# Moving the mask transposes from TensorE to a transposing DMA, the small start loads to GpSimd's queue, and adding a branch hint, in a two-layer graph kernel

## The chip, the cores and the metric

The kernel runs on one core of a Trainium2 chip, in one launch. The metric is the device time of a run in microseconds (us). Engines are named as the profile names them: PE is TensorE (matrix products and transposes), PEld its weight loads, DVE is VectorE, ACT is ScalarE, POOL is GpSimd and SP is SyncE, which here only issues DMAs. A q behind an engine's name (SPq, POOLq) marks what its sequencer does by itself: issuing a DMA, a branch, a wait.

## The reference

There are 64 graphs (B) of 256 nodes (N) with 256 features (D), and an integer mask `adj` per graph, drawn as 0 or 1. Two layers run one after the other on `x`:

```python
x = x + _L0_gnn_ref(_layernorm(x), adj, W, a)          # graph attention under the mask
x = x + _L0_ffn_ref(_layernorm(x), W_in, conv_w, ...)  # a Mamba-2 block: projection, conv, scan, gate, W_out, W_lin
x = x + _L1_gnn_ref(_layernorm(x), adj, adj, weight, bias)   # relational sum: masks (adj == r) @ x, times weight[r]
x = x + _L1_ffn_ref(_layernorm(x), gate_w, ...)        # mixture of 8 experts, one per token, with a capacity
```

The mask is used twice. The attention wants it with a target node on each partition (the way it lies in memory); the relational sum needs it with the source node on the partitions, so each 128x128 block of it has to be transposed. In the relational sum a value r of `adj` selects `weight[r-1]`; with a mask of zeros and ones only relation 1 ever occurs.

## The kernel before, in words

The program is written twice: a fast form that assumes that the mask holds only 0 and 1, and a slow, general form for any integers. The fast form sums up a test of the mask in `tested` while it runs; at the end `again` says whether the general form must run, and an `If` (L1844) skips it otherwise. With these inputs it is skipped.

Each form has two passes.

**First pass.** `prepare` (L583) loads and combines weights: `win` (the Mamba input projection), `wx` (attention weights with extra columns), `wf` (W_out times W_lin with routing columns), `wrel`. The helpers `centred` (L510) and `projected` (L526) do this by PE products whose results DVE (L522, L550) or ACT (L538) copies out of PSUM. `smaller` (L563) loads nine small parameter vectors (`cw`, `cb`, `aneg`, `dtb`, `dch` twice, `blin`, `brel`, `gb`) by DMAs that ACT issues (L566); DVE then halves `cw` and `cb` (L572), and ACT and DVE turn `aneg` into minus its exponential (L638, L639). `clear_slots` (L717) fills the routing table `slots` by another DMA from ACT (L721).

Then 32 groups follow, each of two graphs, which is 512 tokens in four tiles of 128. `group` (L1562) is `attention`, `scan`, `mix`, `relate`, and after every second group `choose`, which routes tokens to experts. In `attention` ACT makes `hide` (L947), a bf16 tile of 128x1024 that is 0 where there is an edge and -2^53 where there is none. In `mix` the same tile, there called `entries`, is transposed by PE, eight 128x128 blocks a group in two steps of four (L1270), into PSUM, and ACT squares and scales it into `adjT`, a 0/1 matrix (L1280). `relate` multiplies by it (L1340, through the helper line L871).

The engines' order in the fast first pass is not the program's order. Every piece of work is a step of a planner (`Plan`, L143): an engine, an estimated duration, what it reads and writes, and for DMAs a latency (`late`) and a time on the shared transfer (`move`). `Plan.record` (L230) simulates the five engines and emits the steps in the order that comes out; ties of start times go by a due time from the tables `DUE` (steps of a group) and `LATE` (steps before and after the groups). Each engine then works through its list in order, so a step that waits holds everything behind it on that engine. SP's list holds the loads of `x` and `adj`, the round trips through DRAM that spread rows over partitions (`s2d` L975/L979, `sumd` L1137, `spread` L1145) and the stores.

```python
            if found is None or t < found[0] - 0.05 or (
                t < found[0] + 0.05 and step.rank < found[1].rank
            ):
                found = (t, step)
```

Near the end of the groups three expert blocks (`first_block`, L1443) fill gaps.

**Second pass** (L1624). Experts' tokens are worked on in blocks of 512 (`wholes`) and of 128 (`quarters`), as many of each as a count found at run time says. Blocks are a nest of `If`s (L1814) inside one another; each block near its end marks a branch hint for the next block's `If` (L1818) on PE, ACT and DVE (`LEAPS`). Before the blocks POOL gathers tokens for the first ones: whole block 0, whole block 1, quarter blocks 0 and 1 (L1807 to L1809), and DVE normalizes quarter block 0 (`ahead`, L1810). Here engines follow the program's order.

Of the kernel before, what the change touches and what calls it, by code (L numbers as in the profile page):

```python
# [20 lines left out]
P = 128  # L21
# [15 lines left out]
    -26698, -26684, 16811, 5376, -1385, 22233, -9147, -5334, -6104, 16470, -4131, -12656,  # L37
    -16678, -3231, 6549, -17865, 6326, -26892, -31112, -17903, -11408, -796, -4422, -12203,
    -5594, 1406, -16327, -16058, -1084, -23798, -1397, -15584, 5401, -4898, -4435, 935, -15679,
    -4926, -36182, -30952, -7116, -5042, -13894, -12081, -3776, -29694, -776, -6149, -737,  # L40
    -14378, -1040, -15690, -8132, 2125, -13292, -19871, -13259, -19271, -17469, 3004, -3551,
    4598, 2717, -5807, -3518, -9626, -6760, -8973, -6760, -21580, -11090, -13187, -7075, -11614,
    8090, 12562, -15384, -25650, -16843, -17448, -16224, -33117, 17100, -11357, -1083, -673,
    -3047, -34625, -12261, -11942, 2714, -6609, 1789, 18383, -20000, 539, -3738, -33183, 333,
    14191, 6307, -9703, 30905, -7622, -19413, -14996, -28968, 116, 19317, 13445, 26060, -32817,
    248, -10405, 2927, -14690, 5944, -2080, -8721, 12774, 2204, -13729, 4024, -22409, -14504,
    5811, -7220, 1399, 13432, 6555, 4744, 7244, -13074, -17598, 12021, -2116, 1124, 383, 10928,
    4031, 2410, 19564, 20208, -4179, 14906, 17031, 1067, -9078, 28505, -6557, -15751, 31775,
    11208, -2943, -655, 18912, 7874, -12175, -12506, -31318, 19350, -32822, -27902, -1902,
    -2614, -22515, -11078, -32731, -7356, 9498, -25579, 6544, -6873, -12295, -8836, -15217,  # L50
    -101, -7100, 1503, -1212, -9384, -7250, 7131, 13184, 2367, 8234, -705, 2385, 15949, -10902,
    -6702, -11680, 4975, -8597, -19533, -14786, 2673, 6442, -7886, -3758, -14584, -18956, -2394,
    6472, -5117, -11835, -8654, 5355, -7098, 108, -26795, -19293, 8894, -21711, 8534, -22778,
    -5174, -16079, -18727, 6779, -14626, -18887, 15787, 204, 5445, -8225, -16055, 4780, 11196,
    -12432, -7396, 2489, -34797, 6092, -3614, -2035, -16485, -22244, -7928, 6163, -16171,
    -13402, 1393, 27308, -3299, 5434, 7440, -6001, 3226, -22066, 7952, -6124, -10687, 10110,
    -11601, -18846, 4084, -3318, -15991, -8790, -25459, 1833, -3473, -2961, -9107, -8293,
    -10502, -18974, -9710, -22513, -11406, -10557, -20206, -7421, -19897, -8699, -9302, -1570,
]
LATE = [  # L60
    -64053, -54702, -59145, -54915, -60062, -63895, -58481, -57817, -56638, -54542, -53887,
    -59553, -60544, -66295, -55138, -53590, -62371, -50547, -58476, -56411, -63929, -54771,
    -63020, -60249, -57757, -55870, -61971, -61584, -58713, -56315, -59515, -60412, -56997,
    -64050, -63593, -58710, -64327, -56974, -64548, -58677, -56261, -55764, -60770, -59294,
    -62214, -59216, -59275, -59000, -57674, -55104, -55629, -58061, -56012, -54911, -56448,
    -55347, -53242, -55651, -59000, -49001, -50233, -59769, -51850, -47995, -48427, -58143,
    -60315, -52513, -54188, -52953, -54782, -51621, -54327, -55185, -53707, -51746, -57084,
    -60544, -52244, -51134, -55346, -54169, -51215, -49728, -43803, -49582, -50567, -47711,
    -54575, -51840, -56142, -59770, -49885, 1346, -2673, -2320, -6355, -808, -6495, -5278,
    -5282, -4565, -4966, -834, -2200, -5069, -7821, -3201, -6160, -4309, -4527, -4910, -2257,  # L70
    -8341, -9201, -6505, -7591, -10768, -9145, -8325, -8954, 8280, 735, 3335, -7607, 7899, 6405,
    7444, -13853, 1045, -3011, 6416, -58, -9653, 9740, 2791, 9305, -3096, 1595, 7797, -2202,
    7339, -6677, 1395, 1189, 3316, 8270, 4320, 8345, 5395, -1209, 1024, 496, 4166, -5572, 10007,
    984, -7144, -1767, -9049, 430, 8168, 10157, 6125, 715, 2433, 5530, 2682, 9681, 4044, -3041,
    -2968, 5666, 3203, 7815, 2227, 4671, 4049, -972, 4835, -9096, 753, -943, -2244, 8804, -7176,
    9169, -3264, 14310, -351, -5008, 8557, -1420, 9011, 5402, 779, 9849, 8608, 3319, 8980, 5929,
    -754, -2251, 3474, -6957, 7127, 2274, 10247, -3481, 49, -3510, -403, -1726, 3946, 2006,
    -1802, 6377, 976, 1673, 5692, 3521, 6, -7831, -15890, 3058, 4170, -7076, 10709, 9000, 6424,
    5864, 2733, 2629, -4870, -702, -2673, 634, -1458, 1299, -687, 5733, -4310, 3394, -1918, 941,
    7852, -2182, 5064, -1684, 13692, 2798, 396, 8917, -2630, 8846, 9132, -2375, 11666, 11022,  # L80
    2337, 10279, 5111, 2075, -596, 5177, -3671, 3927, 3650, 11368, -4611, -3648, -135, -7000,
    2097, 4479, -1495, -2818, 6266, 3575, 372, 3192, -53, 1241, -9215, -13160, 8371, 1767,
    -8809, 9253, 10686, 2871, 6318, 5744, 6064, -7776, -3563, -2652,
# [59 lines left out]
class Plan:  # L143
# [6 lines left out]
    LEFT = 30  # L150

# [34 lines left out]
    def step(self, engine, us, go, reads, writes, late=0.0, port=0, move=0.0):  # L186
        k = self.k.get(self.due, 0)
        self.k[self.due] = k + 1
        due = (DUE if self.due == "group" else LATE)[k]
        step = Step(engine, us, go, self.g, self.TAIL[engine] + late, PACE * self.g + due,  # L190
# [128 lines left out]
def gnn_mamba_rgcn_moe(ctx: ExitStack, tc: tile.TileContext, a: dict, out: bass.AP):  # L319
# [33 lines left out]
    def row(ap):  # L353
        return ap.rearrange("(o d) -> o d", o=1)
# [33 lines left out]
    ident_b = const.tile([P, P], BF16, name="ident_b")  # L388
    nc.vector.tensor_copy(ident_b, ident)
# [92 lines left out]
    def first_pass(form, pass1):  # L482
# [80 lines left out]
        def smaller(s):  # L563

            def load(us, move, dst, src, home):
                s.step(ACT, us, lambda: nc.scalar.dma_start(out=dst, in_=src), [], [home], late=1.5, move=move)  # L566

            dskip = a["L0_ffn_D"].rearrange("(c q) -> q c", q=2)
            load(0.5, 0.2, cw, a["L0_ffn_conv_w"].rearrange("(c p) k -> p c k", p=P), s.fixed(cw))
            load(0.5, 0.2, cb, a["L0_ffn_conv_b"].rearrange("(c p) -> p c", p=P), s.fixed(cb))  # L570
            for half in (cw, cb):
                s.step(DVE, 0.1, lambda half=half: nc.vector.tensor_scalar(  # L572
                    half, half, 0.5, None, ALU.mult), [], [s.fixed(half)])
            load(0.5, 0.1, aneg, row(a["L0_ffn_A_log"]).broadcast_to([P, NH]), s.fixed(aneg))
            load(0.5, 0.1, dtb, row(a["L0_ffn_dt_bias"]).broadcast_to([P, NH]), s.fixed(dtb))
            for q in range(2):
                load(1.4, 0.1, dch[q * 64 : (q + 1) * 64, :], dskip[q : q + 1, :].broadcast_to([64, NCT]),
                     (s.fixed(dch), q))
            load(0.5, 0.5, blin[:, 0:D], row(a["L0_ffn_b_lin"]).broadcast_to([P, D]), (s.fixed(blin), "d"))
            load(0.5, 0.5, brel[:, 0:D], row(a["L1_gnn_bias"]).broadcast_to([P, D]), (s.fixed(brel), "d"))  # L580
            load(0.5, 0.1, gb, row(a["L1_ffn_gate_b"]).broadcast_to([P, E]), s.fixed(gb))

        def prepare(s):  # L583
# [36 lines left out]
            for i in range(2):  # L620
# [4 lines left out]
            s.step(DVE, 0.1, lambda: nc.vector.tensor_copy(gq0()[:, :, E + 1 :], win[:, :, DPROJ - NH :]),  # L625
                   [(win_, "dt")], [(two_, "q2")])
# [11 lines left out]
            s.step(ACT, 0.2, lambda: nc.scalar.activation(aneg, aneg, AF.Exp), [], [rate_])  # L638
# [78 lines left out]
        def clear_slots(s, homes):  # L717

            blank = s.tile("dm", [P, E * CAPP * 4 // P], bufs=4)
            s.step(POOL, 0.7, lambda: nc.gpsimd.memset(blank(), FAR), [], [blank])  # L720
            s.step(ACT, 0.5, lambda: nc.scalar.dma_start(  # L721
                out=slots.rearrange("(p j) w -> p (j w)", p=P), in_=blank()), [blank], homes, late=2.0, move=1.2)
# [457 lines left out]
        def mix(s, g, xe, entries, full, dt, gate, xh, bm, cm, dec):  # L1180
# [82 lines left out]
            adjT = []  # L1263
            for bi in range(2):
                ps, at = s.psum(BF16), s.tile("adjT", [P, 512], F32R, bufs=3)

                def turn(bi=bi, ps=ps):
                    for k in range(2):
                        for h in range(2):
                            nc.tensor.transpose(  # L1270
                                ps()[:, k * N + h * P : k * N + (h + 1) * P],
                                entries()[:, 2 * bi + h, k * P : (k + 1) * P],
                                ident_b,
                            )
# [349 lines left out]
    def second_pass(form, pass2):  # L1624
# [180 lines left out]
        for i in range(2):  # L1805
            quarters.fetch_weights(i)
# [76 lines left out]
```

## Time and profile before

| what | value |
|---|---|
| time, median of 3 runs | 2338.86 us (2333.72, 2338.86, 2339.75) |
| the profiled execution | 2332.68 us; its span from first to last instruction 2331.0 us |
| busy share of the span: PE, PEld, DVE, ACT, POOL | 96%, 67%, 75%, 71%, 39% |
| mean granted TensorE clock | 0.987 |
| moved by DMA | 274.71 MB, mean 118 GB/s |
| first pass | 0 to about 1765 us; steady groups from 60 to 1450 us, 50 us a group |
| second pass | whole blocks to about 2257 us, six quarter blocks to 2310 us |

The page of a profile lists busy times, the span in 40 slices, DMA queues, the chain of work that ended last, and the costliest groups of instructions with the idle time before them and who ended it. Further views of the trace answer narrower questions: who waited for whom, one line's or one tile's instructions, busy times by stage, and instructions in order of time. Matmuls overlap each other, so the duration of one is longer than the step from one to the next.

### The profile page before, as it was taken

How to read it: one execution, taken by the hardware profiler on the slowest of the kernel's cores; microseconds unless marked ns; L12 is line 12 of the kernel's file. 1: busy time of each engine (PE TensorE's matmuls, PEld its weight loads, DVE VectorE, ACT ScalarE, POOL GpSimd, SP SyncE). 2: the span in 40 equal slices, each digit the busy share in tenths (PEclk: the TensorE clock that was granted, in tenths of full speed). 3: DMA queues.
4: the chain of work that ended last, by engine and by line, in shares of the span. 5: the costliest groups of instructions: out<-in, count | busy, mean ns of one | idle time of the engine just before them, and what ended most of it. 6: DMA issues, size and time to landing. Idle time of an engine off the chain costs nothing.

```text
span 2331.0 us, 34861 instructions
## 1 busy us (share of the span) xinstructions
PE 2232.1 (96%) x11079; PEld 1558.4 (67%) x11079; DVE 1757.0 (75%) x4396; ACT 1665.1 (71%) x3864; POOL 919.7 (39%) x994
## 2 busy tenths in 40 slices
PE   5999999999999999999999999999998999999996
PEld 4676766667676666766766667656665666666675
DVE  3899999999999998999998998799654434333342
ACT  3899999899999899999999988888632222222223
POOL 1233435354453445445354444533635222222221
PEclk7999999999999999999999999999999999999998
DMA  4333445444444445444444444424527333333336
GB/s 135 95 90 107 112 117 126 110 108 108 116 121 128 110 102 115 120 118 126 110 108 108 110 123 117 111 67 113 158 81 242 122 119 113 114 117 117 114 92 194
DMA packets 200022, 274.71 MB, mean 118 GB/s; under 512 B 28505, under 2 KB 165919, under 8 KB 199809
## 3 DMA queue, kind: packets, MB, share of 16 engines
q1 hardware_dynamic: 149968, 211.48, 28.9%
q0 software_dynamic: 46848, 58.91, 13.8%
q8 instruction: 93, 1.52, 0.3%
q10 hardware_dynamic: 2992, 1.81, 0.2%
q14 instruction: 121, 0.98, 0.2%
HBM read 187.70 MB, written 46.04 MB: 100 GB/s over the span
## 4 chain that ended last, share of the span: by engine, by line
PE 40%; issue 20%; ACT 12%; POOL 11%; DVE 10%; DMA 5%; SPq 0%; POOLq 0%; ACTq 0%; DVEq 0%
PE ps L871 26%; PE ps L1240 4%; POOL slots L1436 3%; POOL out_dram L477 3%; POOL xg L455 3%; ACT dm L1158 2%; DVE y L1098 2%; PE ps L910 2%; PE ps L1244 2%; PE ps L1543 1%; ACT dm L1164 1%; DMA x<-in_x_dram 1%; DVE dm L1232 1%; ACT xh L1256 1%; ACT xn L925 1%
## 5 line engine op out<-in xcount | busy, mean ns | idle before, releaser
L871 PE MATMUL ps<-xnT,win 128*128 128x512 f32 x1152 | 542.0, 597 | 4.8 <-ACT xnT L915 3.8
L1158 ACT ACTIVATE dm<-spread,cs 128x256 f32<-128x256 f32 (+1 forms) x1024 | 379.3, 452 | 22.6 <-PE ps L1244 22.6
L1098 DVE SCALAR_TENSOR_TENSOR y<-ps,cw,y 128x510 f32<-128x510 f32 (+2 forms) x480 | 351.5, 738 | 34.6 <-ACT y L1091 31.8
L871 PEld LDWEIGHTS ps<-xnT,win 128*128 128x128 f32 x1152 | 205.9, 190 | 171.6 <-issue 150.8
L1744 PE MATMUL ps<-w,hid 128*128 128x256 f32 x1184 | 263.3, 380 | 0.0
L871 PE MATMUL ps<-wf,gate 128*128 128x265 f32 x1024 | 250.8, 388 | 0.0
L1744 PEld LDWEIGHTS ps<-w,hid 128*128 128x128 f32 x1184 | 224.2, 191 | 37.0 <-issue 8.1
L1730 PE MATMUL ps<-xnT,w 128*128 128x512 f32 (+1 forms) x704 | 246.8, 509 | 1.5 <-ACT xnT L1711 1.5
L1232 DVE TENSOR_TENSOR dm<-dm,bc 128x1536 f32<-128x1536 f32 x128 | 225.2, 1760 | 2.5 <-ACT dm L1164 2.4
L871 PEld LDWEIGHTS ps<-wf,gate 128*128 128x128 f32 x1024 | 190.3, 190 | 45.2 <-issue 11.7
L1734 ACT ACTIVATE hid<-ps,b 128x512 f32<-128x512 f32 (+1 forms) x184 | 110.4, 604 | 129.4 <-PE ps L1730 126.1
L1730 PEld LDWEIGHTS ps<-xnT,w 128*128 128x128 f32 x704 | 120.6, 193 | 118.3 <-issue 111.0
L1164 ACT ACTIVATE dm<-dm 128x1536 f32<-128x1536 f32 x128 | 190.5, 1490 | 0.0
L1436 POOL DMA_INDIRECT slots<-meta,sl x128 | 153.8, 1201 | 50.6 <-issue 31.5
L1240 PE MATMUL ps<-dm,xdt 128*64 128x256 f32 x1024 | 169.4, 391 | 3.6 <-DVE xdt L1221 2.9
L889 DVE BATCH_NORM_STATS2 st<-x 128x6 f32<-128x256 f32 x384 | 155.2, 413 | 1.5 <-DMA x<-in_x_dram 1.3
L879 POOL TENSOR_SCALAR ve<-mv 128x4 f32<-128x4 f32 x96 | 36.6, 382 | 300.6 <-DVE mv L892 186.1
L1749 DVE SCALAR_TENSOR_TENSOR yv<-ps,meta,bp 128x256 f32<-128x256 f32 x50 | 24.2, 484 | 160.7 <-PE ps L1744 150.0
L871 PE MATMUL ps<-wrel,hr 128*128 128x265 f32 x512 | 136.1, 395 | 2.0 <-ACT hr L1349 0.5
L871 PE MATMUL ps<-wx,xT 128*128 128x292 f32 x512 | 134.9, 409 | 0.0
L1711 ACT COPY xnT<-ps 128x512 f32<-128x512 f32 (+1 forms) x48 | 21.4, 496 | 152.4 <-PE ps L1708 152.4
L871 PE MATMUL ps<-wh,eT 128*128 128x273 f32 x512 | 126.9, 395 | 0.5 <-ACT eT L1016 0.5
(311 smaller groups left out, 4845.1 us busy)
## 6 DMA issues: line engine op xcount, KB each, us to landing
spread<-sumd SPq DMA_DIRECT2D x128, 512.0 KB, 4.0
w<-in_L_ffn_w_dram SPq DMA_DIRECT2D x50, 1024.0 KB, 6.0
x<-blin POOLq DMA_DIRECT2D x32, 530.0 KB, 5.7
x<-brel POOLq DMA_DIRECT2D x32, 530.0 KB, 5.7
x<-in_x_dram SPq DMA_DIRECT2D x32, 512.0 KB, 5.3
adji<-in_adj_dram SPq DMA_DIRECT2D x32, 512.0 KB, 4.6
out_dram<-x SPq DMA_DIRECT2D x32, 512.0 KB, 3.0
x3d<-x SPq DMA_DIRECT2D x32, 512.0 KB, 6.1
```

The source lines that it names most:

```text
L455: nc.gpsimd.indirect_dma_start(out=dst, out_offset=None, in_=source, in_offset=bass.IndirectOffsetOnAxis(ap=col, axis=0),)
L871: nc.tensor.matmul(out_, lhsT=lhsT, rhs=rhs, start=(i == 0), stop=(i == len(pairs) - 1))
L889: s.step(DVE, 0.34, lambda j=j: nc.vector.bn_stats(sb()[:, j, :], src()[:, j, 0:D]), [(src, j)], [(sb, j)])
L1098: nc.vector.scalar_tensor_tensor(y3[:, :, d:], p3[:, :, : N - d], cw[:, c, k : k + 1], y3[:, :, d:], ALU.mult, ALU.add,)
L1158: nc.scalar.activation(dm()[:, q, bi, o : o + n], spr()[:, q, t1 - n : t1], AF.Relu, bias=cs()[:, 4 * h + j : 4 * h + j + 1], scale=-1.0,)
L1164: s.step(ACT, 1.38, lambda: nc.scalar.activation(dm(), dm(), AF.Exp, scale=-1.0), [], [dm])
L1232: s.step(DVE, 1.67, lambda dm=dm: nc.vector.tensor_mul(dm(), dm(), bc().unsqueeze(1).to_broadcast([P, 2, 2, N + P])), [bc], [dm], port=1)
L1240: nc.tensor.matmul(o, lhsT=xdt()[:, 2 * bi, h * 64 : (h + 1) * 64], rhs=dm()[:, q, bi, 0:N], start=True, stop=False,)
L1436: s.step(POOL, 1.1, lambda j=j: apart("slots", nc.gpsimd.indirect_dma_start(out=slots, out_offset=bass.IndirectOffsetOnAxis(ap=sl()[:, j : ...
L1730: nc.tensor.matmul(ps[:, :n], lhsT=w1[:, k, f * P : (f + 1) * P], rhs=turned[:, k, :], start=(k == 0), stop=(k == 1),)
L1734: nc.scalar.activation(hid[:, f, :], ps[:, :n], AF.Relu, bias=self.b1[i % 2][:, f : f + 1])
L1744: nc.tensor.matmul(ps[:, :D], lhsT=hid[:, f, j * P : (j + 1) * P], rhs=w2[:, f, :], start=(f == 0), stop=(f == NFT - 1),)
```

## The change

Five things change; the rest of the kernel stays.

1. The mask's transposes. The two PE steps a group go, with the PSUM banks they used and the bf16 identity `ident_b`. In their place SP issues one transposing DMA a group from `entries` to a new bf16 tile `turned` in SBUF (one buffer), and ACT's squaring reads `turned` instead of PSUM.
2. The nine small loads go to GpSimd's queue. Halving `cw` and `cb` and the exponential of `aneg` now come after `wx` in their dependences, and so does the DMA that clears `slots`. The columns of `W_in` for `dt` are loaded by a small DMA of their own from SP (in place of a DVE copy out of `win`).
3. The planner counts a PE step 2.2% longer (`SLOWER`), and both tables of due times are new. So the order of all steps of the first pass may differ.
4. In the second pass the gather for whole block 1 is issued before that for whole block 0.
5. Every executed quarter block of the fast form also marks a hint for the general form's branch, as likely taken, on PE, ACT and DVE.

```diff
+    SLOWER = 1.022
...
+        us *= self.SLOWER if engine == PE else 1.0
...
-    ident_b = const.tile([P, P], BF16, name="ident_b")
-    nc.vector.tensor_copy(ident_b, ident)
...
             def load(us, move, dst, src, home):
-                s.step(ACT, us, lambda: nc.scalar.dma_start(out=dst, in_=src), [], [home], late=1.5, move=move)
+                s.step(POOL, us, lambda: nc.gpsimd.dma_start(out=dst, in_=src), [], [home], late=2.0, move=move)
...
-            for half in (cw, cb):
-                s.step(DVE, 0.1, lambda half=half: nc.vector.tensor_scalar(
-                    half, half, 0.5, None, ALU.mult), [], [s.fixed(half)])
...
-            s.step(DVE, 0.1, lambda: nc.vector.tensor_copy(gq0()[:, :, E + 1 :], win[:, :, DPROJ - NH :]),
-                   [(win_, "dt")], [(two_, "q2")])
+            load(0.3, lambda: gq0()[:, :, E + 1 :],
+                 a["L0_ffn_W_in"][:, DPROJ - NH :].rearrange("(k p) o -> p k o", p=P), (two_, "q2"))
...
-            s.step(ACT, 0.2, lambda: nc.scalar.activation(aneg, aneg, AF.Exp), [], [rate_])
+            for half in (cw, cb):
+                s.step(DVE, 0.1, lambda half=half: nc.vector.tensor_scalar(
+                    half, half, 0.5, None, ALU.mult), [wx_], [s.fixed(half)])
+            s.step(ACT, 0.2, lambda: nc.scalar.activation(aneg, aneg, AF.Exp), [wx_], [rate_])
...
-                out=slots.rearrange("(p j) w -> p (j w)", p=P), in_=blank()), [blank], homes, late=2.0, move=1.2)
+                out=slots.rearrange("(p j) w -> p (j w)", p=P), in_=blank()), [blank, s.fixed(wx)], homes,
+                   late=2.0, move=1.2)
...
-            adjT = []
+            adjT, turned = [], s.tile("turned", [P, 2, 2, 2, P], BF16)
+            s.step(SP, 0.4, lambda: nc.sync.dma_start_transpose(
+                out=turned().rearrange("p b h k n -> p (b h k) n"),
+                in_=entries().rearrange("p j n -> p (j n)")), [entries], [turned], late=2.0, move=1.2)
             for bi in range(2):
-                ps, at = s.psum(BF16), s.tile("adjT", [P, 512], F32R, bufs=3)
...
-                s.step(PE, 0.24, turn, [entries], [ps])
...
+                def square(bi=bi, at=at):
+                    out_ = at().rearrange("p (k h n) -> p k h n", k=2, h=2)
+                    in_ = turned()[:, bi].rearrange("p h k n -> p k h n")
...
+                        nc.scalar.activation(
+                            out_, in_, AF.Square, scale=-1.0 / NEG_BIG, bias=one,
+                            accum_out=tested[:, g, 1 + bi : 2 + bi])
...
+        wholes.gather(1, nc.gpsimd)
         wholes.gather(0, None)
-        for blocks, i in ((wholes, 1), (quarters, 0), (quarters, 1)):
-            blocks.gather(i, nc.gpsimd)
+        for i in range(2):
+            quarters.gather(i, nc.gpsimd)
...
                     def hint(k=k, i=i + 1):
+                        if form == "fast" and k:
+                            tc.mark_branch_hint_location("general", "LikelyTaken", engines=LEAPS)
...
-                here.enter_context(tc.If(again > 0))
+                here.enter_context(tc.If(again > 0, label="general"))
```

The two tables of numbers (`DUE` and `LATE`) are left out of the diff; all of their rows are new.

## The prediction

> **What bounds the kernel now.** I read first the busy times of all engines by stage.
>
> ```profile
> core 0: us, PE busy (x) PEld busy (x) DVE busy (x) ACT busy (x) POOL busy (x), PEclk, DMA share, GB/s
> 0.00:16.00 16.00, 7.59 (x20) 4.14 (x20) 2.17 (x20) 0.00 (x0) 2.95 (x17) 1.00 0.54 154
> 16.00:23.00 7.00, 0.00 (x0) 0.00 (x0) 1.97 (x7) 1.49 (x2) 0.00 (x0) 0.70 0.64 189
> 23.00:37.00 14.00, 13.64 (x61) 13.17 (x62) 6.23 (x28) 3.33 (x8) 1.36 (x2) 0.50 0.57 184
> ...
> 60.00:1450.00 1390.00, 1362.24 (x7401) 953.91 (x7400) 1279.92 (x3034) 1265.85 (x3014) 610.31 (x654) 1.00 0.44 112
> 1450.00:1765.00 315.00, 301.50 (x1464) 207.68 (x1463) 238.66 (x620) 213.63 (x499) 140.24 (x148) 0.99 0.42 114
> ```
>
> From 60 to 1450 us PE is busy 98% of the time, DVE 92%, ACT 91%: PE bounds the groups, and only 27.8 us of its time there is waiting. DMA is busy 44%. The start is another matter: for 7 us PE does nothing, then runs at half clock. The waits of the first 60 us say why:
>
> ```profile
> ACT L638 <- DMA cw<-in_L_ffn_conv_w_dram: 19.5, 1, 19.5
> DVE aneg L639 <- ACT aneg L638: 10.7, 1, 10.7
> ...
> PE ps L533 <- DVE gate L522: 8.2, 1, 8.2
> ```
>
> ACT computes nothing before 19.5 us: its list begins with eleven DMA issues, the last of which ends at 19.47 us by the timeline. DVE's list has `aneg` (L639) early, so it stands 10.7 us behind ACT, and the centring copies (L522) behind that make PE wait 8.2 us.
>
> Then the steps that the change takes away, by their line:
>
> ```profile
> L1270 PE MATMUL ps<-ident_b,hide x256: 216/219/230, 46.1 to 1668.6; 128*128 128x128 bf16 x128
> ```
>
> In the timeline a step of four starts 0.234 us before the next step of PE, in nearly all of the 64. And two places of the second pass, the wait at its entry and the branch over the general form:
>
> ```profile
> DVE xn L461 <- DMA xg<-x3d,place: 18.7, 1, 18.7
> ```
>
> ```profile
> L1842 PEldq COMPARE_BRANCH  x1: 4492/4492/4492, 2311.4 to 2311.4; - x1
> ...
> L1842 POOLq COMPARE_BRANCH  x1: 50/50/50, 2319.4 to 2319.4; - x1
> L1842 POOLq INC_SWDGE_SEM  x1: 1597/1597/1597, 2322.5 to 2322.5; - x1
> ```
>
> **The change, part by part.** The sum is made against the profiled execution, 2332.68 us (span 2331.0). The median of the runs, 2338.86, is 6.2 above it; I carry the difference over.
>
> *Mask steps off PE.* 64 x 0.234 = 15.0 us of PE. PE is the bound where they stand, and its successor stands ready almost always (waits 2%). DVE and ACT keep 8 to 9% of room, against 0.47 us of 50 (0.9%) that a group gets shorter. Bounds: 0 (something else sets the pace) and -15.0. I take 7/8 of it, -13, since in the late stage PE waits 4% already.
>
> *What replaces them.* ACT's squaring stays, 64 instructions; it now reads SBUF. The row is L1280, 684 ns from PSUM, against L1256, the same function on 128x512 from SBUF, 632 ns: at most 3 us less on an engine that isn't the bound, counted at nothing. SP gets 32 transposing DMAs of 256 KB. No row shows one. The nearest is `s<-s2d`, also 256 KB onto 128 partitions: issued in 0.34 us, landed in 3.1. The far end is the loads of single 4-byte elements (`dch`: 0.67 us to issue, 8.2 to land for 1 KB). I take the near row, since the operation moves whole tiles. Cover: in steady groups `hide` is done 100 us before PE's first mask step of that group (238.3 against 340.8 us in group 5), so a latency of 3 or of 10 us is hidden alike. It is not hidden from SP's list: behind the transpose stand the loads of `x` and the `s2d` and `spread` trips, and PE waits for `x` six times already between 60 and 1450 us (6.0 us in all). Traffic: 8.4 MB more, on 275, with the engines 44% busy. Taken as 0; the other end is in the second rival.
>
> The Trainium skill ("VectorE: DVE Perf Modes", section on the three transpose paths) speaks against the move: it gives 390 ns for a 128x128 bf16 block on TensorE and 1309 ns by the DMA crossbar, and advises TensorE where PSUM will do. This trace has 0.234 / 4 = 0.06 us a block as PE steps it, even cheaper; no run here shows the crossbar. By the page's figure, an estimate, eight blocks in a row would be 10.5 us a group, under the cover above, and the sum would stay the same unless SP is held meanwhile.
>
> *Small loads to POOL.* ACT loses nine issues, and `clear_slots` moves behind `wx`. POOL gets nine DMAs; its one plain DMA row (L701) is 1.13 us, so 10.2 us, in a stretch (3.6 to 31.8 us) where POOL waits 28.2 us for L701's data. So they end near 14 us; `cw`, `cb`, `dtb` are first needed in the first scan, after 60 us. If that cover were gone, POOL's next step (L879, 36.8 us) would be late by the rest. The extra `dt` load costs SP one issue of 0.37 us and takes a DVE copy of 0.18 us that waited 5.8 us for `win`. With ACT free and `aneg` behind `wx`, DVE's 10.7 us of waiting and with it PE's 8.2 us go, unless the loads of `x` come late: the first is issued at 13.1 us, and PE uses it at 36.3. Bounds: 0 (the new order puts another wait there) and -8.2 by this row; if the clock also held, PE's 16 us at half clock (23 to 39 us) could lose up to half, 7 to 8 more, so -16. I take -8.
>
> On that last item the skill ("TensorE: Matmul & The Clock Gate", part 1) says that an idle window of about 3.4 us halves the clock. The rows agree: PE rests from 15.2 to 23.4 us and its granted clock is 0.50 afterwards. By that rule the start would give the whole -16; I hold to -8, as other short waits may do the same.
>
> *The new order.* Tables and `SLOWER` change every tie. The trace can't show the new waits; it can bound them: all of the 27.8 us gone, or as much again, so -28 to +28. I take 0, and this is the widest term.
>
> *Gather order.* DVE's 18.7 us wait at the second pass's entry is for quarter block 0's gather (`ahead`, L1810), which is the ninth of ten before and after. Whole block 1's rows come four gathers (4 x 1.27 = 5.1 us) earlier, but their normalization stands behind `ahead` on DVE. So 0; -5 if `ahead` is not what it waits for.
>
> *Hint.* Six quarter blocks ran. A hint costs 28 ns on PE (23 of them stand in the trace already): 6 x 0.03 = 0.2 us. What could it give? PE spends 4.49 us in the branch (L1842), but PE, ACT and DVE are through at 2316.4, 2317.5 and 2320.5 us, and POOL, which gets no hint, branches at 2319.4, goes on at 2322.0 and drains to 2330.1. POOL sets the end, so the gain is 0. The far side: if each early hint pushes out code that the next block needs, up to 4.49 us a block, 27 us.
>
> Sum: -13 - 8 + 0.2 = -20.8. 2332.7 - 20.8 = 2311.9, on the median's scale 2338.9 - 20.8 = **2318**.
>
> **Rivals.**
> - *The PE time goes into waits* (no change). The group's pace is taken over by DVE and ACT, or the new order waits 15 to 20 us more, inside the bound of +28. For it: DVE and ACT at 92% and 91%. Against: 8% is much more than 0.9%. Time: -20.8 + 18 = -3, some 2336.
> - *SP becomes the place of the loss* (slower). A transpose holds SP's list, or the DMA rings behind it, longer than 0.34 us, and the `x`, `s2d` and `spread` transfers behind it come late to PE. It decides from 20.8 / 32 = 0.65 us of PE waiting a group. At 2 us a group it is +64, so 2338.9 - 20.8 + 64 = 2382; at the 8 us of the small-element row held each time, +256. For it: no row shows the operation, and PE already waits for `x`. Against: SP spends most of its time waiting, and the 100 us of slack lets the planner place it anywhere.
> - *The hint hurts*: +27 at most on top, 2345. Against: 23 hints in the trace, with whole blocks at 100% PE from 1800 to 2245 us; but those name branches that are mostly not taken.
> - *Better than forecast*: the clock holds at the start and all of the mask steps count: -15 - 16 = -31, 2308; with a good order below 2303.
>
> **How the numbers follow.** The measurement can tell about 0.3%, 7 us. Forecast, including the better case, 2300 to 2331: 0.61. Waits, 2332 to 2346: 0.13. SP, or the hint, above 2346: 0.26. The likeliest case alone would be 2302 to 2331. Leaving out 5% below and 15% above gives 2302 to 2362. Faster 0.61, same 0.13, slower 0.26.
>
> **What would show it.** Right: L1270 gone, groups 49.5 to 49.7 us apart instead of 50.1; ACT's first instruction before 5 us, PE's first group product (L871, now 42.2 us) near 34; SP's new issues under 0.5 us; the span's end still on POOL. Wrong: PE waits for `x`, `s` or `spread` in each group; SP issues of several us; the period unchanged with more PE waits; quarter blocks longer than 7.8 us apart.

## The result, and the profile after

The changed kernel takes 2342.91 us (median of 20 runs) against 2336.44 us of the kernel before (20 runs): a ratio of 1.0032, 95% interval 1.0024 to 1.0040. It is 7 us slower, where 21 us less was forecast. The profiled execution has a span of 2341.0 us (2331.0 before).

Busy time by stage, kernel after; the columns are PE, PE's weight loads, DVE, ACT and POOL busy in us, the granted clock, the DMA share and GB/s:

```profile
core 0: us, PE busy (x) PEld busy (x) DVE busy (x) ACT busy (x) POOL busy (x), PEclk, DMA share, GB/s
...
16.00:23.00 7.00, 6.25 (x47) 5.71 (x46) 4.80 (x22) 2.00 (x7) 0.90 (x1) 0.95 0.89 296
23.00:37.00 14.00, 11.28 (x54) 9.60 (x54) 6.92 (x26) 7.44 (x16) 3.23 (x7) 0.90 0.56 167
...
60.00:1450.00 1390.00, 1348.74 (x7093) 933.21 (x7093) 1306.64 (x2989) 1252.40 (x2987) 610.87 (x645) 0.99 0.47 116
```

At the start PE works from 16 to 23 us, where it did nothing before, and its clock is 0.90 instead of 0.50 from 23 to 37 us. In the first 60 us there is one long wait of PE in the group steps, for ACT's `ev`, which was 5.6 us before:

```profile
PE ps L1011 <- ACT ev L1000: 9.6, 1, 9.6
```

From 60 to 1450 us PE has less work, as foreseen, but the work takes longer to pass: DVE is busy 26.7 us more with almost the same instructions. Where the time went is best seen in the times at which stages begin (first matrix product of the stage in each trace, us from the span's start; "old order" is the whole change with the steps in their old order, `all_old_order` below):

| stage begins | before | after | whole change, old order |
|---|---|---|---|
| group 0 (its first decay sum, L1126 before) | 76.2 | 63.1 | 72.7 |
| group 4 | 235.1 | 230.7 | 230.9 |
| group 24 | 1236.1 | 1246.0 | 1230.9 |
| first whole block | 1764.1 | 1780.4 | 1757.3 |
| second whole block | 1802.8 | 1811.8 | 1796.8 |
| first quarter block | 2261.8 | 2272.9 | 2256.2 |
| end of the span | 2331.0 | 2341.0 | 2323.1 |

The period is the distance from group 4 to group 24, divided by 20: 50.05 us before, 50.77 us after, 50.00 us with the old order. All periods below are made in this way. The distances alternate (46.0 and 53.7 us before), so a pair of groups, some 100 us, is the unit in which work repeats.

The transposing DMA has a row of its own, from the instructions of its line (minimum, median and maximum of its issue on SP's list, in ns):

```profile
L1266 SPq DMA_TRANSPOSE turned<-hide x32: 1252/2024/3894, 32.1 to 1645.8; - x32
```

At the end, the branch over the general form is no shorter for PE (5.2 us, 4.49 before); POOL branches last, 0.2 us behind DVE:

```profile
L1845 PEldq COMPARE_BRANCH  x1: 5203/5203/5203, 2324.2 to 2324.2; - x1
...
L1845 POOLq COMPARE_BRANCH  x1: 50/50/50, 2331.7 to 2331.7; - x1
```

### The profile page after: what moved, and what is told of

It is laid out like the page before. It is cut to its first block, busy times and chain, and to the rows that moved or that the text cites. A ratio compares the mean times of both kernels' runs of the same rounds, so it can differ in the third digit from the quotient of the medians.

```text
span 2341.0 us, 34444 instructions
## 1 busy us (share of the span) xinstructions
PE 2233.4 (95%) x10823; PEld 1545.8 (66%) x10823; DVE 1802.1 (77%) x4394; ACT 1662.8 (71%) x3864; POOL 933.4 (40%) x1003
## 5 line engine op out<-in xcount | busy, mean ns | idle before, releaser
L1100 DVE SCALAR_TENSOR_TENSOR y<-ps,cw,y 128x506 f32<-128x506 f32 (+2 forms) x480 | 354.3, 741 | 28.3 <-ACT y L1093 26.3
L1234 DVE TENSOR_TENSOR dm<-dm,bc 128x1536 f32<-128x1536 f32 x128 | 235.1, 1836 | 7.0 <-ACT dm L1166 6.0
L873 PEld LDWEIGHTS ps<-wf,gate 128*128 128x128 f32 x1024 | 196.3, 194 | 65.9 <-issue 19.8
L881 POOL TENSOR_SCALAR ve<-mv 128x4 f32<-128x4 f32 x96 | 51.7, 538 | 321.8 <-DVE mv L894 320.4
L891 DVE BATCH_NORM_STATS2 st<-x 128x6 f32<-128x256 f32 x384 | 150.1, 416 | 6.9 <-DMA x<-in_x_dram 6.2
L873 PE MATMUL ps<-wx,xT 128*128 128x292 f32 x512 | 145.8, 422 | 0.0
L873 PE MATMUL ps<-wh,eT 128*128 128x273 f32 x512 | 132.6, 402 | 3.6 <-ACT eT L1018 3.5
L873 PE MATMUL ps<-wrel,hr 128*128 128x265 f32 x512 | 130.6, 392 | 3.6 <-ACT hr L1349 2.9
L1093 ACT ACTIVATE y<-ps,cb,cw 128x512 f32<-128x512 f32 x160 | 123.6, 772 | 10.7 <-PE ps L873 10.5
```

Of the source, the lines that this page charges most:

```text
L873: nc.tensor.matmul(out_, lhsT=lhsT, rhs=rhs, start=(i == 0), stop=(i == len(pairs) - 1))
L891: s.step(DVE, 0.34, lambda j=j: nc.vector.bn_stats(sb()[:, j, :], src()[:, j, 0:D]), [(src, j)], [(sb, j)])
L1093: s.step(ACT, 0.66, lambda: nc.scalar.activation(y(), ps(), AF.Identity, scale=cw[:, c, 3:4], bias=cb[:, c : c + 1]), [ps, s.fixed(cw), s. ...
L1100: nc.vector.scalar_tensor_tensor(y3[:, :, d:], p3[:, :, : N - d], cw[:, c, k : k + 1], y3[:, :, d:], ALU.mult, ALU.add,)
L1234: s.step(DVE, 1.67, lambda dm=dm: nc.vector.tensor_mul(dm(), dm(), bc().unsqueeze(1).to_broadcast([P, 2, 2, N + P])), [bc], [dm], port=1)
```

## The experiments

Eighteen kernels. The ratio is to the kernel before in the same job (its medians there: 2334.2 to 2335.8 us). A time is the median of 4 to 12 runs. The four kernels without a time leave out work on which the routing of tokens depends; they ran once each, and only their period is read.

| kernel | time, us | ratio (95%) | period, us |
|---|---|---|---|
| dma_old_order | 2334.00 | 1.0003 (0.9994 to 1.0012) | 49.92 |
| start_old_order | 2327.53 | 0.9968 (0.9958 to 0.9978) | 50.15 |
| second_pass | 2335.88 | 1.0002 (0.9992 to 1.0011) | 50.11 |
| all_old_order | 2326.57 | 0.9969 (0.9958 to 0.9980) | 50.00 |
| no_turn_old_order | 2337.40 | 1.0013 (1.0002 to 1.0023) | 49.87 |
| plain_copy | 2359.18 | 1.0101 (1.0084 to 1.0118) | 51.15 |
| no_accum | 2334.51 | 0.9998 (0.9989 to 1.0008) | 50.06 |
| no_accum_dma | 2330.63 | 0.9983 (0.9974 to 0.9993) | 49.87 |
| no_adds_new_order | (routing changed) | | 49.96 |
| no_adds_old_order | (routing changed) | | 49.92 |
| short_trip | (routing changed) | | 49.97 |
| short_trip_dma | (routing changed) | | 49.89 |
| slots_later_dma | 2312.98 | 0.9907 (0.9892 to 0.9922) | 49.26 |
| slots_later_pe | 2318.55 | 0.9933 (0.9919 to 0.9946) | 49.65 |
| slower1 | 2425.93 | 1.0397 (1.0381 to 1.0413) | 53.03 |
| slots_all_later | 2349.99 | 1.0062 (1.0049 to 1.0076) | 51.05 |
| plain_copy_old | 2337.98 | 1.0019 (1.0009 to 1.0029) | 49.88 |
| slots_behind_both | 2310.56 | 0.9898 (0.9880 to 0.9917) | 49.38 |

Periods of kernels that do not touch the groups differ by up to 0.1 us (50.05, 50.11, 50.15), so less than that is not read.

### The parts one by one, in the old order

The planner's order comes out of its costs and tables, so any edit of a step changes the order of all others. These four kernels keep the planner as in the kernel before: it plans the old steps, and only what a step emits is changed.

```diff
 # dma_old_order, shortened: the PE step stays in the plan and emits nothing
-                s.step(PE, 0.24, turn, [entries], [ps])
+                s.step(PE, 0.24, lambda: None, [entries], [ps])
 # after the mask of group g is made and group g-1's is squared
+                nc.sync.dma_start_transpose(
+                    out=turned[0].rearrange("p b h k n -> p (b h k) n"),
+                    in_=entries().rearrange("p j n -> p (j n)"))
```

> The kernel before, every step in its old order, with the mask steps alone replaced: a transposing DMA of SP per group in place of the eight PE transposes, issued as soon as the mask is made and the squaring of the group before is done; ACT squares from SBUF. No other part of the change. Theory O (the new order of the steps is what costs the time; the transposing DMA as such is covered): the groups come 49.5 to 49.7 us apart instead of 50.05, the time falls by 11 to 15 us, to 2321 to 2326 us. Theory D (the transposing DMA itself, by its 2 us on SP's list or by its traffic, slows the groups): 50.5 to 50.8 us apart as in the kernel after, the time rises by 14 to 23 us, to 2350 to 2360 us.

Measured: 2334.0 us, no change; period 49.92 us. Neither theory: the DMA does not cost 14 us, but PE's 15 us are not gained either. Where they went is in the waits of PE in 20 steady groups, first before, then here:

```profile
PE ps L1009 <- ACT ev L998: 10.5, 20, 0.9
PE ps L910 <- DMA x<-in_x_dram: 4.5, 5, 1.6
PE ps L871 <- DVE x L1312: 0.2, 1, 0.2
```

```profile
PE ps L1014 <- ACT ev L1003: 10.8, 21, 0.9
PE ps L870 <- DVE x L1330: 4.4, 10, 0.5
PE ps L909 <- DMA x<-in_x_dram: 3.1, 3, 1.4
```

A new wait for DVE's `x` has come, 0.44 us once in a pair. In the intervals from one matrix product to the next the steps around `ev`, `seen`, `wf` and `xlo` are together 0.44 us a group longer, while those of `bm` are 0.11 shorter. So of the 0.467 us a group that PE no longer works, 0.33 have gone into longer intervals between its other products.

```diff
 # start_old_order, shortened: the old places in the plan
-                s.step(ACT, us, lambda: nc.scalar.dma_start(out=dst, in_=src), [], [home], late=1.5, move=move)
+                s.step(ACT, us, lambda: nc.gpsimd.dma_start(out=dst, in_=src), [], [home], late=1.5, move=move)
 # halvings, rate and the clearing of the slots: emitted behind the last column of wx
```

> The kernel before, steps in the old order, with the edits of the start alone: the small loads issued by GpSimd at the places where ACT issued them, the halvings, the rate and the clearing of the slots behind the last column of wx, and the dt columns loaded by SP instead of copied by DVE. Forecast (term of -8, bounds 0 and -16): the first group product starts 8 to 13 us earlier and the time falls by 8 to 13 us, to 2323 to 2328 us. Rival (the earlier start is eaten in the first groups, as the kernel after lost 8.7 of its 13.1 us between its first and its fifth group): within 4 us of before, 2332 to 2337 us.

Measured: 2327.5 us, 7.5 us less (0.0032 of 2335), just under the forecast 8 to 13. The first group product starts at 34.0 us instead of 42.2, and group 0 is 7.1 us earlier, group 4 7.0, the first whole block 6.2, the end 7.7: the gain is kept to the end. The granted clock from 23 to 37 us is 0.99 here.

Where the 8.2 us at the first group product come from can be read from PE's timeline, first before, then here (start, duration):

```profile
23.36 1.09 PE L533 MATMUL ps<-ident,wx 128*128 128x128 f32 x4 [8.19 <-DVE gate L522]
```

```profile
21.83 1.06 PE L533 MATMUL ps<-ident,wx 128*128 128x128 f32 x4
```

The first product behind the old wait starts only 1.5 us earlier. From it to the first group product PE works through the same products in both kernels, in 18.8 us before and in 12.1 us here. So 6.7 of the 8.2 us come in the stretch whose clock rose.

second_pass is the diff's edits of the second pass (gathers and hint) on the kernel before.

> The kernel before with the two edits of the second pass alone: the new order of the gathers and the hint. By the trace of after (first whole block 31.4 us long instead of 38.7; the way from the last whole block to the first quarter block 2.2 us longer; the end 2.8 us nearer to PE's last product): 5 to 8 us less, 2328 to 2331 us. By the forecast (gathers 0, hint +0.2): 2336 to 2337 us. If the hint hurts: above 2339 us.

Measured: 2335.9 us, no change, as forecast. PE's time in the last branch is 4.75 us with the six hints, 4.49 without (one profiled execution each). The shorter first whole block of the kernel after (31.4 us) does not come from the gathers: here it is 38.0 us long.

> The whole change, but with the steps of the first pass in the old order (old tables, PE durations not scaled): the sum of the three kernels beside it. Theory O: -11 to -15, -8 to -13 and -5 to -8 add up, 2300 to 2314 us; the change without its new order is as good as forecast or better. Theory D: the groups stay 50.5 us apart or more and the time is 2335 to 2350 us, about that of after.

Measured: 2326.6 us, in neither theory's range: theory O had counted 11 to 15 us for the mask steps, which gave none. The three ratios multiplied give 0.9973, and 0.9969 was measured: the parts add up. So **the new order alone takes the kernel from 0.9969 to 1.0032 (each known to about 0.001): 14.7 us of 2335**.

### Why PE's freed time was no gain

Two edits shorten the loop of a pair at places that its chain of waits names: ACT's squaring, and the trip of the row sums through memory. no_accum leaves out the sums that ACT's squaring gives (`accum_out`), once with PE's mask steps and once with the DMA; no_turn_old_order leaves out the DMA.

> As the kernel with the old order and the transposing DMA, but without that DMA: ACT squares the mask as it lies, so the mask of the second layer is not turned (left out: the transposition). Theory L (the period of the groups is set by a loop over PE, ACT, the s2d trip, GpSimd and DVE, on which only half of the mask steps lay; the DMA costs nothing): as with the DMA, 49.9 us a group and 2331 to 2337 us. Theory D (PE would have gained its 0.47 us a group, and the transposing DMA takes it back): 49.5 to 49.6 us a group, 2319 to 2325 us.

> The kernel before, PE mask steps and order as they were, with ACT's squaring of the masks made shorter: it gives no sums (left out: the count that tests the masks' entries; the second accumulator read of 0.2 us per squaring goes). ACT loses 64 x 0.2 = 12.8 us, PE nothing. Theory L (ACT's runs lie on the loop that sets the period): 0.1 to 0.2 us a group less, 2328 to 2332 us. Theory P (PE at 98% sets the period): no change, 2333 to 2337 us.

> The same shorter squaring on ACT together with the transposing DMA in place of PE's mask steps, old order. Theory L (two nearly equal paths, PE's and ACT's; either one alone gains little): together 0.3 to 0.5 us a group less, 2319 to 2326 us. Theory D (the transposing DMA takes back what PE gains): no better than the shorter squaring alone.

Measured: without the DMA 1.0013, 49.87 us a group, so the transposing DMA costs nothing here. A shorter squaring gains nothing alone; with the DMA it gains 4 us, but the period (49.87 us) is that of the DMA alone (49.92 us), so the 4 us do not come from the steady groups; where they come from stays open. ACT's squaring does not lie on the loop of the groups.

```diff
 # short_trip, short_trip_dma
-                out=s2(), in_=line.broadcast_to([P, 4 * P])), [line_], [s2], late=1.4, move=1.2)
+                out=s2(), in_=row(a["L0_ffn_conv_b"][0 : 4 * P]).broadcast_to([P, 4 * P])), [line_], [s2], late=1.4, move=1.2)
```

> The kernel before, with the trip of the attention's row sums through memory cut short: the row that comes back to all partitions is read from an input that is always there, so it needn't wait for the row that was just written (left out: the right row sums; routing changes, so only the period is read). Theory C (the chain of a pair of groups: PE, an ACT run, the two transfers of this trip of 7 us in all, GpSimd, DVE, ACT, PE; this loop sets the period and not PE's 98%): the first leg of 2.1 us falls out of the loop once in two groups, and the period goes from 50.05 to 49.0 to 49.6 us. Rival P (PE sets it): 50.0 to 50.1 us.

> The same short trip with the transposing DMA in place of PE's mask steps, old order. Theory C: with the loop shorter PE comes nearer to being the bound, and now the 0.47 us of its mask steps show: 0.2 to 0.5 us a group less than the short trip alone. Rival P: 0.13 us less, as without the short trip.

Measured: 49.97 and 49.89 us; theory C fell as well. But the chain of waits of this kernel shows what is late next when the trip is short (start in us, duration, what):

```profile
479.86 0.33 POOL slots L1436
...
483.23 0.97 POOL slots L1436
484.20 0.30 issue
484.51 0.97 POOL slots L1436
485.48 0.30 issue
485.78 2.12 POOL slots L1436
...
490.49 1.07 POOL r2r L1309
...
491.58 0.56 DVE x L1312 x2
```

Seven of a pair's eight indirect writes of the routing table `slots`, most of them 0.97 us with 0.30 us between, stand on POOL's list ahead of L1309, where POOL makes `r2r`, a reciprocal root of 128x4 numbers. DVE waits for that root 25.4 or 25.5 us in 20 groups, in the kernel before, in dma_old_order and in short_trip alike:

```profile
DVE x L1312 <- POOL r2r L1309: 25.4, 10, 2.6
```

So four kernels move these writes on POOL's list.

```diff
 # slots_later, shortened: noted(j) is the indirect write of row j as it was;
 # j >= 3 (first 12 pairs) is kept back and emitted at the next group's mask additions
-                s.step(POOL, 1.1, lambda j=j: noted(j), [sl, meta],
+                s.step(POOL, 1.1, lambda j=j: s.later.append(lambda: noted(j)) if held and j >= 3 else noted(j),
+                    [sl, meta],
```

> The whole change in the old order, and on GpSimd's list the last five of the eight indirect writes of slots of each pair of groups (first 12 pairs) are moved behind the two mask additions of the next group, so the root of L1309 (r2r, for which DVE waits 25.4 us in 20 groups) no longer stands behind them. Theory Q (with the row-sum trip cut, the chain went through these writes: GpSimd's list is the loop that sets the old order's period, and it hid what PE gained): DVE's wait for r2r goes to nearly nothing and the groups come 49.0 to 49.6 us apart; 2303 to 2318 us. Rival M (many loops of nearly the same length): 49.8 to 50.0 us, 2322 to 2328 us.

> The same with PE's mask steps kept: start, gathers and hint of the change, old order, slots moved on GpSimd's list, no transposing DMA. Theory Q: 49.4 to 49.8 us a group, 0.3 to 0.47 us more than with the transposing DMA beside it, since PE is now the bound; 2315 to 2323 us. Rival M: 50.0 to 50.1 us, 2325 to 2329 us.

Measured: 2313.0 us with the transposing DMA, 2318.6 us with PE's mask steps; periods 49.26 and 49.65 us. Theory Q holds. With these writes out of the way, taking the mask steps off PE is worth 0.385 us a group of the 0.467 that they take. In the whole run it is worth 5.6 us of the 15.0. With the writes in their old place the same edit was worth 0.15 us a group and 1 us in all (start_old_order against all_old_order). PE in 990 us of steady groups, with the DMA:

```profile
230.00:1220.00 990.00, 979.72 (x5235) 688.02 (x5234) 923.05 (x2228) 920.75 (x2203) 447.90 (x490) 1.00 0.53 122
```

> As the kernel with the transposing DMA and the late slots (2313 us), with all eight indirect writes of slots of a pair behind the next group's two mask additions, not only the last five. There DVE waits 12.2 us in 20 groups for the mask additions (hm), which still stand behind three of the writes. Theory Q: that wait goes, PE waits less, 49.0 to 49.2 us a group, 2308 to 2312 us. Rival M: PE is now the bound (979.7 of 990 us busy), no change, 2312 to 2315 us.

Measured: 2350.0 us, 37 us worse than with five late writes. The timeline of POOL showed why: the late writes came between the two additions of a group's mask, not behind both: four in slots_later_dma, seven here, ahead of the second. DVE's wait here:

```profile
DVE ev L1028 <- POOL hm L1013: 43.2, 10, 4.5
```

> The trace showed that the two kernels before placed the late writes between the two mask additions (four of them in the kernel of 2313 us, seven in the one of 2350 us, where DVE waits 43.2 us in 20 groups for the second addition). Here all eight stand behind both additions; else as before: the whole change in the old order. Theory Q (what stands on GpSimd's list ahead of r2r and the mask additions sets the period until PE does): DVE's wait for the mask additions falls from 12.2 (2313 us) and 43.2 us to below 3 us, 49.0 to 49.2 us a group, 2307 to 2312 us. Rival M: no better than 2313 us, 49.26 us a group.

Measured: 2310.6 us, 1.0% below the kernel before. That is the lowest median, but its interval overlaps that of slots_later_dma (2313.0 us), whose period is shorter; the two can't be told apart. The wait for the mask additions is gone, but the period is 49.38 us, not 49.0 to 49.2: the writes now stand ahead of the next group's root on POOL, for which ACT, and behind it DVE, waits:

```profile
DVE xlo L1373 <- ACT xhi L948: 12.5, 10, 1.3
...
ACT xhi L948 <- POOL rs L903: 13.7, 10, 1.4
```

These writes, five or all eight of a pair, at three new places on POOL's list give three periods between 49.26 and 51.05 us, against 50.00 in the old place. POOL is busy 44 to 48% of the time in these kernels, and yet what stands ahead of what on its list changes the pace.

### Why the new order is slower

> The kernel after, in its new order, with the transposing DMA replaced by a plain copy of the same 256 KB from and to the same tiles (left out: the transposition of the mask). Theory O (the new order of the steps costs the time): the issue on SP falls from 2.0 to some 0.35 us, and the time stays at 2339 to 2346 us, 50.7 us a group. Theory D2 (in the new order the transposing DMA hurts, by 2 us on SP's list or by its many small packets): 50.0 to 50.2 us a group, 2322 to 2330 us.

> The kernel before in its old order with the mask steps replaced by a plain copy of 256 KB per group issued by SP (left out: the transposition). In the new order the plain copy was slower than the transposing DMA (51.15 against 50.77 us a group). If a plain copy as such is dearer for the transfers beside it: 50.2 to 50.4 us a group, 2340 to 2350 us, against 49.92 us and 2334 us with the transposing DMA. If that was only where the new order puts it on SP's list: 49.9 us, 2332 to 2336 us.

Measured: 2359.2 us in the new order, so taking the transposition out gains nothing there; 2338.0 us in the old. The issue on SP is 0.48 us for the plain copy and 2.02 (new order) or 1.63 us (old order) for the transposing DMA, and the shorter issue is the slower kernel in the new order by 16 us. Theory O's number was missed, theory D2 fell. Why a plain copy at that place of SP's list is worse stays open.

What the new order does show is DVE. The same instructions, by shape, in 1015 us of the kernel before and of the kernel after (busy us, mean ns):

```profile
L1232 DVE TENSOR_TENSOR dm<-dm,bc 128x1536 f32<-128x1536 f32 x82 | 143.5, 1750 | 0.0
L1048 DVE TENSOR_TENSOR dv<-x,rs 128x32 f32<-128x32 f32 x20 | 4.5, 227 | 0.0
```

```profile
L1234 DVE TENSOR_TENSOR dm<-dm,bc 128x1536 f32<-128x1536 f32 x81 | 151.7, 1872 | 4.8 <-ACT dm L1166 4.5
L1050 DVE TENSOR_TENSOR dv<-x,rs 128x32 f32<-128x32 f32 x20 | 23.4, 1171 | 0.0
```

An instruction on 128x32 elements takes 1171 ns in the mean, and the timeline of DVE and of POOL tells when (start, duration):

```profile
462.53 2.50 DVE L1050 TENSOR_TENSOR dv<-x,rs 128x32 f32<-128x32 f32 x1
464.95 0.21 DVE L1402 TENSOR_TENSOR lg<-lg,lmx 128x64 f32<-128x64 f32 x1
```

```profile
462.31 1.36 POOL L922 DMA_DIRECT2D x<-brel  x1
463.19 1.79 POOL L1260 TENSOR_TENSOR xh<-xh 128x512 f32<-128x512 f32 x1
```

`dv` ends with POOL's addition of two tiles, at 465.0 us, and all of DVE's list stands behind it. This comes in eight of the ten pairs of the stretch, at the same place each time. I took, for each DVE instruction in 20 groups, its duration above the lower quartile of its kind (from 60 ns up) and put it down to the POOL instruction that overlaps it most. This excess is 12.0 us before, of which 5.2 under `xh<-xh`; 12.7 and 5.6 us in all_old_order; 47.7 and 45.1 us after. Of the 47.7 us, `dv`, `dm` and `dt` take 37.5. The test leaves these additions out:

```diff
 # no_adds, shortened (one of two edits): the three additions of squares per group, steps kept in the plan
-                s.step(POOL, 1.3, lambda c0=c0: nc.gpsimd.tensor_add(
-                    sq()[:, c0 + 1, :], sq()[:, c0 + 1, :], sq()[:, c0, :]), [(xh, c0)], [(xh, c0 + 1)], port=1)
+                s.step(POOL, 1.3, lambda: None, [(xh, c0)], [(xh, c0 + 1)], port=1)
```

> The kernel after, in its new order, without GpSimd's three additions of squares per group (left out: three of the four parts of the sum that scales the scan's result; the routing of tokens changes with it, so only the groups' period is read, fifth to 25th group). Theory S (the new order lays these additions over DVE's work, which is held meanwhile: DVE's instructions are 47.7 us longer than their usual duration in 20 groups, 45.1 of it while such an addition runs, against 12.0 and 5.2 before): the excess falls below 6 us and the groups come 49.9 to 50.3 us apart instead of 50.77. Rival O (the new order's waits are its own): 50.5 us or more.

> The control: the whole change in the old order, without the same additions. Theory S: little to gain, 49.8 to 50.0 us a group (50.00 with them). Rival O: as much gained here as in the new order, 49.3 to 49.6 us.

Measured: the period falls from 50.77 to 49.96 us in the new order and from 50.00 to 49.92 in the old, which is less than is read; the excess is 2.2 us in the new. The first whole block starts at 1756.7 and 1753.9 us instead of 1780.4 and 1757.3: of the 23.1 us between the orders 2.8 are left. Theory S holds for these two orders.

```profile
L1050 DVE TENSOR_TENSOR dv<-x,rs 128x32 f32<-128x32 f32 x20 | 6.7, 335 | 0.0
```

Leaving the additions out also makes POOL's list shorter, which could itself be the gain. The waits speak against it: in 20 groups of the kernel after, DVE waits 2.1 us for POOL, ACT 0.6 and PE not at all, against some 15 us lost. Some of the waiting for DVE goes instead, such as ACT's for the step behind `dv`, first after, then in no_adds_new_order:

```profile
ACT ex L1403 <- DVE lg L1402: 20.1, 9, 2.6
```

```profile
ACT ex L1401 <- DVE lg L1400: 2.6, 8, 0.4
```

PE's waits for DVE's `run` and `oh` (4.7 and 2.6 us after) are gone with it. no_adds_new_order still has the transposing DMA on SP, so that DMA isn't the loss in the new order either.

The Trainium skill ("SBUF — State Buffer", section "SBUF: two separate sides") says that DVE and GpSimd share one pair of ports as an exclusive lock, which a DVE instruction with two SBUF inputs needs when GpSimd's reads SBUF; the other waits for the whole instruction. The trace agrees in whom it hits most: `dv`, `dm` and `dt` read two tiles in SBUF, while the taps of the convolution, which read PSUM, are as long as before (738 and 741 ns in the mean). It doesn't tell who held the ports first: by the records `dv` begins 0.66 us before the addition, while POOL issues a DMA. That issue alone holds it little: in no_adds_new_order `dv` starts under the same issue and lasts 0.32 us.

```diff
-    SLOWER = 1.022
+    SLOWER = 1.0
```

> The kernel after with its own tables, but PE's durations not scaled by 1.022 in the planning: another order of the same steps. Theory S (an order costs by how much it lays GpSimd's additions over DVE's work): the period rises above 49.95 us by about as much per group as half of DVE's excess over 12 us in 20 groups; with 10 to 60 us of excess, 49.9 to 51 us a group and 2322 to 2350 us. If the scaling itself is the loss: below 2328 us.

Measured: 2425.9 us, 53.03 us a group, excess 31.8 us. Theory S alone does not give that, since the excess is below the 47.7 us of the kernel after: the groups are 23 to 83 us apart, and PE waits for many things in turn, for none more than 11.3 us in 20 groups. The tables belong to the scaled durations; another order of the same steps can cost 83 us more than the one in the kernel after, by other means than DVE's meetings with POOL. By which stays open.

## Why the prediction was wrong, step by step

- **Mask steps off PE, -13: wrong, 0.** The step that failed is "PE is the bound where they stand, and its successor stands ready almost always". PE was busy 98% and still not the bound: a loop over POOL's list, DVE, ACT and PE had the same length to within 0.3%. The bound of 0 ("something else sets the pace") is what came: 0.13 us a group, and no time that could be told from nothing. It could have been read: the chain of waits of the kernel before, from 440 to 541 us, has only two of the four mask steps of a pair on it (0.24 us a group, about half of the term) and runs for some 45 of the 101 us outside of PE.

```profile
440.63 0.24 PE ps L1270 x4
...
490.96 0.97 POOL slots L1436
...
493.22 1.08 POOL r2r L1309
...
494.32 0.56 DVE x L1312 x2
...
516.96 0.24 PE ps L1270 x4
```

- **The new order, 0: wrong, +14.7**, within the bounds of 28. It was called the widest term, and then counted at nothing. That its bounds came from PE's waits alone was the second error: slower1 lies at +93 us, and the loss came through DVE's durations (45.1 us longer in 20 groups under POOL's additions, 5.2 before), which the sum took as fixed.
- **Start, -8: the number right (-7.5 in the old order), its make-up luck.** The sum took all 8.2 us from PE's wait and nothing from the clock. In start_old_order the wait gave 1.5 us and the stretch at the higher clock 6.7. In the kernel after that first product starts 7.9 us earlier (15.4 us) and the stretch behind it is 5.1 us shorter, so the first group product starts at 29.2 us (34 foreseen); but 8.7 of the 13.1 us at group 0 are gone by group 4, where start_old_order keeps its 7.0. ACT's first instruction starts at 1.33 us (under 5 foreseen, 19.5 before), but that is the loading of a table, as it was before; its first copy starts at 12.6 us.
- **Transposing DMA on SP, 0: right, for a wrong reason.** The issue is 1.6 to 2.0 us in the median, not 0.34: the near row was the wrong one. SP's list has the room, as the cover said. The rival that made it the place of the loss is out: no PE wait for `s` or `spread` came, and PE's waits for `x` fell from 4.5 to 3.4 us in 20 groups. ACT's wait for `s` did grow in the new order, from 1.3 to 11.5 us, but it is 10.3 us in no_adds_new_order too, where the loss is gone. The skill's advice against the move ("VectorE: DVE Perf Modes", section "Rules for kernel authors": TensorE for a 128x128 transpose where PSUM will do) is not borne out here: with POOL's writes moved, the groups are 49.26 us apart by DMA and 49.65 by PE.
- **ACT's squaring from SBUF, 0: right.** It takes 715 ns, not 632, against 684 from PSUM: 64 times 30 ns more, on an engine where 12.8 us less gained nothing.
- **Gathers 0 and hint +0.2: right** (1.0002 together). POOL still branches last. The last quarter blocks are 7.8 to 8.2 us apart (7.8 to 8.7 before). The hint does not shorten PE's branch.
- **Rivals.** "The PE time goes into waits" is what happened to the mask steps; its second clause, a new order that waits 15 to 20 us more, is what came on top. I had both as one case against the start's gain. With the measured terms the sum is 0 - 7.5 + 0 + 14.7 = +7.2, and +6.5 to +7.5 was measured. That is no test of the order's term, which was itself had as the difference between the kernel after and the old order.

The best versions found keep the other four parts, drop the new order, and move POOL's indirect writes: 2310.6 and 2313.0 us.

## What to carry to other kernels

An engine at 98% is the bound only if the loop that returns to it is longest through that engine. Follow the chain of waits over one period and count which of the removed instructions lie on it. Here the removal was worth 0.13 to 0.15 us a group while another loop set the pace, and 0.385 of its 0.467 us once that loop was cut. Where an edit makes a planner deal out a new order, measure the edit in the old order first: here the order cost twice as much as any part of the change gained.

## What the runs showed of the hardware that was not expected

- A DVE instruction of 0.19 us that reads two SBUF tiles lasted 2.50 us while POOL issued a DMA and added two tiles, and 0.32 us while POOL only issued that DMA. In 20 groups DVE's instructions were 45 us longer under such additions.
- The transposing DMA of a 128x1024 bf16 tile held its issuing queue for 1.2 to 3.9 us (a plain copy of the same bytes 0.48 us in the median), and no landing is recorded for it.
- Eight indirect writes in a row held POOL's list for 11.6 us (slots_behind_both, 482.9 to 494.5 us). A root of 1.07 us behind seven of them kept DVE waiting some 2.5 us in each pair.
